# A third Strassen-Winograd step for one more product, and another pair of banks for a small product with ones, in an fp32 kernel on one core

## The chip, the cores and the metric

The kernel runs on one core of a Trainium2 chip. The metric is the device time of the program in microseconds (us). Of the kernel before there are three timed runs, with a median of 429.25 us (429.12 to 429.49), and one profiled execution. A change of less than 0.2% counts as no change here.

## The reference

`x` is 8 sequences of 256 rows of 1024 values. Two layers are added to it, each on its own result:

```python
x = x + _L0_cond_ref(x, itok_B_0_7, W, Wr, A, B)
x = x + einsum('bsi,boi->bso', x, weight[itok_B_0_15])
```

Layer one is a dense product `x @ W.T` (2048 x 1024 by 1024 x 1024) plus a low-rank part: router logits with a bias of 5 on the expert that a sequence's language id names, the two best of eight experts weighted by a softmax, and the projections through `A` and `B` (rank 16 each), times 2. Layer two picks one 1024 x 1024 matrix out of 16 for each sequence by its adapter id. All of it is fp32.

## The kernel before, in words

**Layer one.** The dense product, with an identity added to `W` for the residual, is cut by two Strassen-Winograd steps. The outer step makes seven products out of halves of `W` and `x`; they are called `opening("1", ...)` and `product` with the keys 5, 2, 6, 3, 7, 4, in this order (lines 760 to 816). So key 4 is the last product of layer one, and `adapt(0)`, the first sequence of layer two, comes straight after it. The inner step makes seven products again, P1 to P7, inside `opening` and `product`: `a(i, j)` and `b(i, j)` are quarters of the weight and of the x operand, `s1..s3`, `t1..t3` are their sums on VectorE (`make_subs`), and `late` turns `s2`, `t2` into the fourth sums. Each of the seven goes through `mm` (line 442): two contraction steps times two halves of 128 output rows, each call a matmul of 128 weights' columns by 512 columns. The calls with a third string argument ("0", "1", "d") add the low-rank part with two more such calls, from `hg` and `b_sb` or `bdiff`. P2 is `a(0, 0) b(0, 0)`, P1 is `a(0, 1) b(1, 0)`, and the last one, P4, is `a(1, 1) t2` (line 586).

In keys 5, 2, 3 and 4 (`further` true) P1 is cut a third time: seven matmuls of 128 by 256 columns (helper `deep`, line 513) take the place of four of 512. Their operands `r1..r4`, `q1..q4` are small VectorE sums in pool `sub3`, one buffer for each tag, where `r3`, `q3` take the buffers of `r1`, `q1`. Two of the seven have single banks of their own (`A3`, `B3`), three go straight into the accumulator `X`, and the parts are put together in `dest[:, 0]` by `evict` and `add` on VectorE (lines 547 to 578).

**PSUM.** Eight banks: three pairs, called by the roles A, X and B, and two single banks. `roles` turns the pairs round from one product to the next: the next product's A, X and B are the pairs that were X, B and A. So the pair that key 4 calls A is the B of `adapt(0)`, whose first write into it is `mm("B", s1, w["12"], True)` on line 686.

**Order.** The instruction streams are written out by hand (`manual_schedule`); each engine works through its own in order. VectorE work that is not tied to a product lies in the list `todo` and is given out by `pump(place)`, in shares that depend on what `todo` holds alone; `pump(7)` empties it. For key 4 the list holds the preparation of the first adapter's weights (`prep_w1`) and the y sums (`prep_y`).

**The opening.** `opening` starts TensorE while the loads come in. Its X is in pair 0, its A in pair 1. Warm-up matmuls write `idle`, a tile in pair 2, and so does the product of `ones` with the language ids (line 484), which lays the ids over all partitions. `use_ids` reads it on VectorE (line 200, the comparison that makes `bias`). Then B takes pair 2, and `mm(B, s1, t1)` follows on TensorE.

**Queues.** Weights and x come in over SyncE's DMA queue, in program order; the loads for layer two (`load_w1`) overwrite x and weight blocks and wait until these have been read.

Of the kernel before, what the change touches and what calls it, by code (L numbers as in the profile page):

```python
# [9 lines left out]
F32 = mybir.dt.float32  # L10
# [6 lines left out]
P = 128  # L17
# [8 lines left out]
def kernel(  # L26
# [320 lines left out]
    def us(n):  # L347
        return (n + 151) / 960
# [13 lines left out]
        return pieces(fn, wb[out_], wb[x], wb[y], 2)  # L362

    subs = {}

    def make_subs(key, w, x, further=True):

        def a(i, j):  # L370
            return wb[w][:, 2 * j : 2 * j + 2, i * OQ : (i + 1) * OQ]

        def b(i, j):
            return xb[x][:, 2 * i : 2 * i + 2, j * TQ : (j + 1) * TQ]


        ra = lambda i, j: a(0, 1)[:, j, ts(i, P)]
        rb = lambda i, j: b(1, 0)[:, i, ts(j, TQ // 2)]
        t = {}

        def op3(name, tag, fn, x, y, first=4):
            width = P if name[0] == "r" else TQ // 2

            def run():
                t[name] = sub3.tile([P, width], F32, name=f"{name}_{key}", tag=tag)
                fn(t[name], *(t[v] if isinstance(v, str) else v for v in (x, y)))

            return us(width), first, run

        deep = [  # L390
            op3("r1", "r13", add, ra(1, 0), ra(1, 1)),
            op3("q1", "q13", minus, rb(0, 1), rb(0, 0)),
            op3("r2", "r2", minus, "r1", ra(0, 0)),
            op3("q2", "q2", minus, rb(1, 1), "q1"),
            op3("r4", "r4", minus, ra(0, 1), "r2"),
            op3("q4", "q4", minus, rb(1, 0), "q2"),
        ]

        def deep3():
            for o in (  # L400
                op3("r3", "r13", minus, ra(0, 0), ra(1, 0)),
                op3("q3", "q13", minus, rb(1, 1), rb(0, 1)),
            ):
                o[2]()

        def op(name, fn, x, y, first):
            pool = sub2 if name[1] == "2" else sub1
            width = OQ if name[0] == "s" else TQ

            def run():  # L410
                t[name] = pool.tile([P, 2, width], F32, name=f"{name}_{key}", tag=name)
                fn(t[name], *(t[v] if isinstance(v, str) else v for v in (x, y)))

            return us(2 * width), first, run

        def late_s():
            minus(t["s2"], a(0, 1), t["s2"])

        def late_t():
            minus(t["t2"], b(1, 0), t["t2"])  # L420

        subs[key] = (a, b, t, (late_s, late_t), (ra, rb, deep3), further)
        return [
            op("s1", add, a(1, 0), a(1, 1), 3),
            op("t1", minus, b(0, 1), b(0, 0), 3),
            op("s2", minus, "s1", a(0, 0), 3),
            op("t2", minus, b(1, 1), "t1", 3),
            op("s3", minus, a(0, 0), a(1, 0), 5),
            op("t3", minus, b(1, 1), b(0, 1), 5),
        ] + (deep if further else [])  # L430

    def evict(dest, acc, base=None):

# [24 lines left out]
    def opening(key, dest):  # L458


        idle = pair("idle", 2)
        for i in range(WARM):
            nc.tensor.matmul(idle[:, 0, :P], lhsT=ident, rhs=ident, start=True, stop=True)  # L463
        mm = multiply()
        sums_of = make_subs(key, "11", "11", False)
        a, b, t, late, _, _ = subs.pop(key)
        X = pair(f"X_{key}", 0)
        A = pair(f"A_{key}", 1)
        add_identity(wb["11"], 0, 2)
        mm(X, a(0, 1), b(1, 0), True, part=(0,))  # L470
        project(0, 0, singles("ps_h_0_0"), (2,), last=False)
        mm(X, a(0, 1), b(1, 0), part=(1,))
        evict(dest[:, 0], X)
        project(0, 0, None, (3,), False, False)
        mm(A, a(0, 0), b(0, 0), True, part=(0,))
        project(0, 0, None, (0,), False, False)
        mm(A, a(0, 0), b(0, 0), part=(1,))
        project(0, 0, None, (1,), False, False)
        use_adapter_ids()
        add_identity(wb["11"], 2, 4)  # L480
        for s in sums_of[:4]:
            s[2]()
        add(dest[:, 0], A, dest[:, 0])
        nc.tensor.matmul(idle[:, 1, :NB], lhsT=ones, rhs=ids_f[:, :NB], start=True, stop=True)
        use_ids(idle[:, 1, :NB])
        B = pair(f"B_{key}", 2)
        mm(B, t["s1"], t["t1"], True)
        evict(dest[:, 3], B)
        for s in sums_of[4:]:
            s[2]()  # L490
        mm(A, t["s2"], t["t2"])
        evict(dest[:, 1], A)
        project(0, 0, None, range(KH, KC), False)
        take(0, 0)
        for f in late:
            f()
        mm(A, t["s3"], t["t3"])
        add(dest[:, 3], A, dest[:, 3])
        mm(B, t["s2"], b(1, 1))
        add(dest[:, 1], B, dest[:, 1])  # L500
        mm(A, a(1, 1), t["t2"])
        evict(dest[:, 2], A)

    def product(key, base, dest, lora=None, tokens=None):

        a, b, t, late, (ra, rb, deep3), further = subs.pop(key)
        mm = multiply(dict(zip("01d", b_part(lora))) if lora is not None else None, tokens)
        new = roles(key)
        old = [base[:, q] if base is not None else None for q in range(4)]
        n0, n1 = (slice(j * (TQ // 2), (j + 1) * (TQ // 2)) for j in range(2))  # L510

        def deep(acc, lhs, rhs, first=False):
            nc.tensor.matmul(acc, lhsT=lhs, rhs=rhs, start=first, stop=True, skip_group_check=True)  # L513

        def quarter(m, n):

            return dest[:, 0][:, m, n], old[0][:, m, n] if base is not None else None

        A = new("A")
        mm(A, a(0, 0), b(0, 0), True)  # L520
        X = new("X")
        nc.scalar.copy(X, A)
        if not further:
            pump(1)
            B = new("B")
            mm(B, t["s1"], t["t1"], True, "1", 1)
            evict(dest[:, 3], B, old[3])
            pump(3)
            mm(A, t["s2"], t["t2"])
            evict(dest[:, 1], A, old[1])  # L530
            pump(3)
            mm(X, a(0, 1), b(1, 0), False, "0", 0)
            late[0]()
            late[1]()
            evict(dest[:, 0], X, old[0])
            pump(4)
            mm(A, t["s3"], t["t3"])
            add(dest[:, 3], A, dest[:, 3])
            pump(5)
            mm(B, t["s2"], b(1, 1), False, "d", 1)  # L540
            add(dest[:, 1], B, dest[:, 1])
            pump(6)
            mm(A, a(1, 1), t["t2"], False, "1", 0)
            evict(dest[:, 2], A, old[2])
            pump(7)
            return
        A3 = single(f"A3_{key}", 0)[:, n0]
        deep(A3, ra(0, 0), rb(0, 0), True)
        q, o = quarter(0, n0)
        evict(q, A3, o)  # L550
        pump(1)
        B = new("B")
        mm(B, t["s1"], t["t1"], True, "1", 1, ms=(0,))
        B3 = single(f"B3_{key}", 1)[:, n0]
        deep(B3, t["r1"], t["q1"], True)
        deep3()
        mm(A, t["s2"], t["t2"])
        evict(dest[:, 1], A, old[1])
        deep(A3, t["r2"], t["q2"])
        q, o = quarter(0, n1)  # L560
        evict(q, A3, o)
        late[0]()
        pump(2)
        mm(B, t["s1"], t["t1"], True, "1", 1, ms=(1,))
        evict(dest[:, 3], B, old[3])
        late[1]()
        pump(3)
        deep(X[:, 0, n0], ra(0, 1), rb(1, 0))
        deep(X[:, 0, n1], t["r4"], rb(1, 1))
        deep(X[:, 1, n0], ra(1, 1), t["q4"])  # L570
        mm(X, None, None, False, "0", 0, part=())
        deep(A3, t["r3"], t["q3"])
        two = [P, 2, TQ // 2]
        d1 = dest[:, 0][:, 1, :].rearrange("p (j n) -> p j n", j=2)
        both = A3.unsqueeze(1).to_broadcast(two)
        evict(d1, both, old[0][:, 1, :].rearrange("p (j n) -> p j n", j=2) if base is not None else None)
        add(dest[:, 0][:, :, n1], B3.unsqueeze(1).to_broadcast(two), dest[:, 0][:, :, n1])
        add(dest[:, 0], X, dest[:, 0])
        pump(4)
        mm(A, t["s3"], t["t3"])  # L580
        add(dest[:, 3], A, dest[:, 3])
        pump(5)
        mm(B, t["s2"], b(1, 1), False, "d", 1)
        add(dest[:, 1], B, dest[:, 1])
        pump(6)
        mm(A, a(1, 1), t["t2"], False, "1", 0)
        evict(dest[:, 2], A, old[2])
        pump(7)
# [285 lines left out]
```

## Time and profile before

| What | Value |
|---|---|
| Median of the timed runs | 429.25 us |
| The profiled execution's own time | 430.16 us |
| Its span, first to last instruction | 428.4 us |
| Mean granted TensorE clock | 0.999 |
| TensorE (PE) busy | 423.1 us, 99% |
| VectorE (DVE) busy | 281.7 us, 66% |
| ScalarE (ACT) busy | 39.6 us, 9% |

The profile calls the engines PE (matmul), PEld (TensorE's weight load), DVE, ACT, POOL and SP. One `nc.tensor.matmul` of fp32 is two matmul records and two weight-load records. The recorded length of a matmul overlaps the next one, so the time that one costs is read from the distance between starts. L217 is the line of the helper through which all VectorE sums go, L447 the matmul of `mm`, L513 that of `deep`, L660 that of layer two's `mm`, and L435 ScalarE's copy. In a timeline each line is start, length, engine, line, operation, output<-input and count, with the idle time before it in brackets where there was some.

### The profile page before, as it was taken

Reading aid. Unit: us, or ns where it says so; the run is one execution under the profiler, and the core shown is the slowest. Engines: PE = TensorE matmul, PEld = TensorE weight load, DVE = VectorE, ACT = ScalarE, POOL = GpSimd, SP = SyncE. Lnnn points to the kernel's source line nnn. Section 1 sums busy time; section 2 is a strip of 40 time slices with the busy share of each in tenths; the row PEclk is TensorE's granted clock in tenths of the full one; section 3 lists DMA queues with packets and bytes.
Section 4 is the critical chain, followed back from the end, with each engine's and each line's share of the span. In section 5 each row is a group of like instructions: output and inputs, shape, how many; then the busy total and the mean of one; then the engine's idle time right before and its main releaser. Section 6 shows DMA issues by size and latency. Waiting matters only on the chain.

```text
span 428.4 us, 3335 instructions
## 1 busy us (share of the span) xinstructions
PE 423.1 (99%) x1246; PEld 217.3 (51%) x1246; DVE 281.7 (66%) x375; ACT 39.6 (9%) x65; POOL 2.0 (0%) x10
## 2 busy tenths in 40 slices
PE   8999999999999999999999999999999999999996
PEld 5566984545444445444454444444444444444574
DVE  1627288956988959889595676565756576565531
ACT  1120022110000000000000101010110101010110
POOL 1000000000000000000000000000000000000000
PEclk9999999999999999999999999999999999999999
DMA  8995000000000140630302276556748385550202
GB/s 279 383 398 217 2 0 2 0 0 2 0 0 0 31 168 0 249 142 0 99 0 98 98 262 227 199 207 208 272 148 313 128 275 214 196 197 0 98 2 99
DMA packets 14305, 55.83 MB, mean 130 GB/s; under 512 B 1232, under 2 KB 3536, under 8 KB 9808
## 3 DMA queue, kind: packets, MB, share of 16 engines
q1 hardware_dynamic: 12976, 54.68, 35.5%
q10 hardware_dynamic: 1248, 0.93, 0.7%
q8 instruction: 10, 0.16, 0.2%
q14 instruction: 7, 0.06, 0.0%
q0 software_dynamic: 64, 0.00, 0.0%
HBM read 47.22 MB, written 8.39 MB: 130 GB/s over the span
## 4 chain that ended last, share of the span: by engine, by line
PE 98%; DVE 0%; POOL 0%; issue 0%; ACT 0%; POOLq 0%; DVEq 0%
PE A L447 24%; PE A L660 22%; PE B L447 14%; PE B L660 13%; PE ps_h L245 7%; PE X L660 6%; PE X L447 4%; PE A_last L718 3%; PE A L513 1%; PE X L513 1%; PE idle L463 1%; PE ps_g L315 0%; PE B L513 0%; DVE y L217 0%; ACT z L748 0%
## 5 line engine op out<-in xcount | busy, mean ns | idle before, releaser
L660 PE MATMUL B<-x,x 128*128 128x512 f32 x128 | 57.5, 592 | 0.0
L447 PE MATMUL A<-t,s 128*128 128x512 f32 x112 | 50.3, 592 | 0.0
L217 DVE TENSOR_TENSOR y<-A,y 128x1024 f32<-128x1024 f32 (+2 forms) x27 | 26.3, 985 | 25.1 <-PE A L447 14.2
L660 PE MATMUL A<-w,x 128*128 128x512 f32 x88 | 39.6, 592 | 0.0
L660 PEld LDWEIGHTS B<-x,x 128*128 128x128 f32 x128 | 24.3, 190 | 29.8 <-issue 29.7
L217 DVE TENSOR_TENSOR w<-w,w 128x1024 f32<-128x1024 f32 x24 | 29.0, 1223 | 15.4 <-PE A L660 15.3
L660 PE MATMUL A<-w,y 128*128 128x512 f32 x88 | 39.1, 592 | 0.0
L447 PEld LDWEIGHTS A<-t,s 128*128 128x128 f32 x112 | 21.2, 190 | 22.9 <-issue 22.5
L245 PEld LDWEIGHTS ps_h<-y,x 128*128 128x128 f32 x256 | 30.7, 191 | 3.3 <-issue 3.3
L245 PE MATMUL ps_h<-y,x 128*128 128x136 f32 x256 | 30.6, 279 | 0.0
L660 PEld LDWEIGHTS A<-w,x 128*128 128x128 f32 x88 | 16.7, 190 | 21.0 <-issue 21.0
L660 PEld LDWEIGHTS A<-w,y 128*128 128x128 f32 x88 | 16.7, 190 | 21.0 <-issue 21.0
L435 ACT COPY z<-A 128x512 f32<-128x512 f32 x21 | 12.3, 586 | 158.3 <-PE A L660 158.3
L447 PE MATMUL B<-t,s 128*128 128x512 f32 x56 | 25.9, 594 | 0.3 <-DVE bias L200 0.3
L447 PE MATMUL A<-x,w 128*128 128x512 f32 x56 | 25.3, 592 | 0.0
L447 PE MATMUL A<-t,w 128*128 128x512 f32 x56 | 25.2, 592 | 0.0
L447 PE MATMUL B<-x,s 128*128 128x512 f32 x56 | 25.2, 592 | 0.0
L217 DVE TENSOR_TENSOR y<-B,y 128x1024 f32<-128x1024 f32 (+1 forms) x16 | 17.4, 1090 | 9.5 <-PE B L447 8.7
L217 DVE TENSOR_TENSOR x<-x,x 128x1024 f32<-128x1024 f32 (+1 forms) x20 | 19.2, 1004 | 0.0
L447 PEld LDWEIGHTS B<-x,s 128*128 128x128 f32 x56 | 10.6, 190 | 13.4 <-issue 12.7
L447 PEld LDWEIGHTS A<-t,w 128*128 128x128 f32 x56 | 10.6, 190 | 13.4 <-issue 12.7
L217 DVE TENSOR_TENSOR z<-X,z 128x512 f32<-128x512 f32 x8 | 5.5, 692 | 17.9 <-PE X L660 15.9
(119 smaller groups left out, 446.3 us busy)
## 6 DMA issues: line engine op xcount, KB each, us to landing
x<-w_dram SPq DMA_DIRECT2D x24, 1024.0 KB, 4.8
w<-w_dram SPq DMA_DIRECT2D x8, 1024.0 KB, 4.8
out_dram<-z SPq DMA_DIRECT2D x15, 512.0 KB, 3.0
x<-xT_dram SPq DMA_DIRECT2D x6, 1024.0 KB, 12.9
w<-wT_dram SPq DMA_DIRECT2D x3, 1024.0 KB, 14.9
x<-xT_dram SPq DMA_DIRECT2D x4, 256.0 KB, 3.8
x<-xT_dram SPq DMA_DIRECT2D x2, 512.0 KB, 7.4
w<-w11T_dram SPq DMA_DIRECT2D x1, 512.0 KB, 6.1
```

Of the source, the lines that this page charges most:

```text
L217: nc.vector.tensor_tensor(out_, x, y, op)
L245: nc.tensor.matmul(ps[v][:, u * EA : (u + 1) * EA], lhsT=xk(k, j, c)[:, ts(r, P)], rhs=aw_sb[:, k, :], start=(first and k == some[0] and u ...
L435: nc.scalar.copy(dest, acc)
L447: nc.tensor.matmul(acc[:, m, :], lhsT=l, rhs=r, start=(first and i < len(ms)), stop=(i >= len(steps) - len(ms)), skip_group_check=True,)
L463: nc.tensor.matmul(idle[:, 0, :P], lhsT=ident, rhs=ident, start=True, stop=True)
L513: nc.tensor.matmul(acc, lhsT=lhs, rhs=rhs, start=first, stop=True, skip_group_check=True)
L660: nc.tensor.matmul(accs[name], lhsT=lhs[:, k // 2, k % 2, :], rhs=rhs[:, k, :], start=(first and k == 0), stop=(k == KH - 1), skip_group_c ...
L718: nc.tensor.matmul(acc, lhsT=lhs[:, k // 2, k % 2, :], rhs=rhs[:, k, ts(v, m)], start=(first and k == 0), stop=(k == KH - 1), skip_group_c ...
```

## The change

In P4 of key 4 the third step is applied as it is in P1. The code of the third step moves from `make_subs` and `product` into a function `third`; the keys 5, 2 and 3 keep their instructions and their order. In `opening` the product of ones with the ids goes to a new tile `wide` in pair 0, which the opening's first X has left.

```diff
+    NQ = TQ // 2
+
+    def third(key, lhs, rhs):
+        ra = lambda i, j: lhs()[:, j, ts(i, P)]
+        rb = lambda i, j: rhs()[:, i, ts(j, NQ)]
+        n0, n1 = slice(0, NQ), slice(NQ, TQ)
...
+        ops = [
+            op("r1", "r13", add, A(1, 0), A(1, 1)),
+            op("q1", "q13", minus, B(0, 1), B(0, 0)),
+            op("r2", "r2", minus, "r1", A(0, 0)),
+            op("q2", "q2", minus, B(1, 1), "q1"),
+            op("r4", "r4", minus, A(0, 1), "r2"),
+            op("q4", "q4", minus, B(1, 0), "q2"),
+        ]
+
+        def ops3():
+            op("r3", "r13", minus, A(0, 0), A(1, 0))[2]()
+            op("q3", "q13", minus, B(1, 1), B(0, 1))[2]()
+
+        def piece(n, acc=None):
+            if n in (1, 5):
+                own[n] = single(f"P{n}_{key}", n // 5)[:, n0]
+            out_, l, r = {
+                1: lambda: (own[1], ra(0, 0), rb(0, 0)),
+                2: lambda: (acc[:, 0, n0], ra(0, 1), rb(1, 0)),
+                3: lambda: (acc[:, 0, n1], t["r4"], rb(1, 1)),
+                4: lambda: (acc[:, 1, n0], ra(1, 1), t["q4"]),
+                5: lambda: (own[5], t["r1"], t["q1"]),
+                6: lambda: (own[1], t["r2"], t["q2"]),
+                7: lambda: (own[1], t["r3"], t["q3"]),
+            }[n]()
+            nc.tensor.matmul(out_, lhsT=l, rhs=r, start=(n in (1, 5)), stop=True, skip_group_check=True)
+
+        def take(n, dest, base=None):
+            cut = lambda v: {1: v[:, 0, n0], 6: v[:, 0, n1], 5: v[:, :, n1]}[n]
+            if n == 7:
+                cut = lambda v: v[:, 1, :].rearrange("p (j n) -> p j n", j=2)
+            src = own[5 if n == 5 else 1]
+            if n in (5, 7):
+                src = src.unsqueeze(1).to_broadcast([P, 2, NQ])
+            evict(cut(dest), src, None if base is None else cut(base))
+
+        return ops, ops3, piece, take
...
-        nc.tensor.matmul(idle[:, 1, :NB], lhsT=ones, rhs=ids_f[:, :NB], start=True, stop=True)
-        use_ids(idle[:, 1, :NB])
+        wide = pair("ids_wide", 0)[:, 0, :NB]
+        nc.tensor.matmul(wide, lhsT=ones, rhs=ids_f[:, :NB], start=True, stop=True)
+        use_ids(wide)
         B = pair(f"B_{key}", 2)
         mm(B, t["s1"], t["t1"], True)
...
+        two = key == "4"
+        _, ops3, piece, take = deep
...
+        piece(7)
+        take(7, dest[:, 0], old[0])
+        take(5, dest[:, 0], dest[:, 0])
+        if two:
+            ops, ops3, piece, take = third(f"{key}b", lambda: a(1, 1), lambda: t["t2"])
+            for o in ops:
+                o[2]()
         add(dest[:, 0], X, dest[:, 0])
         pump(4)
         mm(A, t["s3"], t["t3"])
         add(dest[:, 3], A, dest[:, 3])
+        if two:
+            piece(1)
+            take(1, dest[:, 2], old[2])
         pump(5)
         mm(B, t["s2"], b(1, 1), False, "d", 1)
+        if two:
+            piece(5)
+            ops3()
+            piece(6)
+            take(6, dest[:, 2], old[2])
         add(dest[:, 1], B, dest[:, 1])
         pump(6)
+        if two:
+            mm(A, None, None, False, "1", 0, part=())
+            for n in (2, 3, 4):
+                piece(n, A)
+            piece(7)
+            take(7, dest[:, 2], old[2])
+            take(5, dest[:, 2], dest[:, 2])
+            add(dest[:, 2], A, dest[:, 2])
+            pump(7)
+            return
         mm(A, a(1, 1), t["t2"], False, "1", 0)
         evict(dest[:, 2], A, old[2])
         pump(7)
```

More of the change, by code (lines that the diff above doesn't have):

```diff
@@ L364, with op, run @@
     subs = {}
+    NQ = TQ // 2
[3 more added lines that the diff above has]
+        n0, n1 = slice(0, NQ), slice(NQ, TQ)
+        t, own = {}, {}
+        def op(name, tag, fn, x, y):
+            width = P if name[0] == "r" else NQ
+            def run():
+                t[name] = sub3.tile([P, width], F32, name=f"{name}_{key}", tag=tag)
+                fn(t[name], *(t[v] if isinstance(v, str) else v() for v in (x, y)))
+            return us(width), 4, run
+        A, B = (lambda i, j: lambda: ra(i, j)), (lambda i, j: lambda: rb(i, j))
+        ops = [
[31 more added lines that the diff above has]
+        return ops, ops3, piece, take
     def make_subs(key, w, x, further=True):
@@ L374, in b @@
             return xb[x][:, 2 * i : 2 * i + 2, j * TQ : (j + 1) * TQ]
-        ra = lambda i, j: a(0, 1)[:, j, ts(i, P)]
-        rb = lambda i, j: b(1, 0)[:, i, ts(j, TQ // 2)]
         t = {}
[L381 to L404, printed above, removed]
         def op(name, fn, x, y, first):
@@ L420, in late_t @@
             minus(t["t2"], b(1, 0), t["t2"])
-        subs[key] = (a, b, t, (late_s, late_t), (ra, rb, deep3), further)
+        deep = third(key, lambda: a(0, 1), lambda: b(1, 0)) if further else None
+        subs[key] = (a, b, t, (late_s, late_t), deep)
         return [
@@ L429, in make_subs @@
             op("t3", minus, b(1, 1), b(0, 1), 5),
-        ] + (deep if further else [])
+        ] + (deep[0] if further else [])
     def evict(dest, acc, base=None):
@@ L465, in opening @@
         sums_of = make_subs(key, "11", "11", False)
-        a, b, t, late, _, _ = subs.pop(key)
+        a, b, t, late, _ = subs.pop(key)
         X = pair(f"X_{key}", 0)
@@ L504, in product @@
     def product(key, base, dest, lora=None, tokens=None):
-        a, b, t, late, (ra, rb, deep3), further = subs.pop(key)
+        a, b, t, late, deep = subs.pop(key)
         mm = multiply(dict(zip("01d", b_part(lora))) if lora is not None else None, tokens)
@@ L509, in product @@
         old = [base[:, q] if base is not None else None for q in range(4)]
[L510 to L517, printed above, removed]
         A = new("A")
@@ L522, in product @@
         nc.scalar.copy(X, A)
-        if not further:
+        if deep is None:
             pump(1)
@@ L546, in product @@
             return
[L547 to L550, printed above, removed]
+        two = key == "4"
+        _, ops3, piece, take = deep
+        piece(1)
+        take(1, dest[:, 0], old[0])
         pump(1)
@@ L553, in product @@
         mm(B, t["s1"], t["t1"], True, "1", 1, ms=(0,))
-        B3 = single(f"B3_{key}", 1)[:, n0]
-        deep(B3, t["r1"], t["q1"], True)
-        deep3()
+        piece(5)
+        ops3()
         mm(A, t["s2"], t["t2"])
         evict(dest[:, 1], A, old[1])
-        deep(A3, t["r2"], t["q2"])
-        q, o = quarter(0, n1)
-        evict(q, A3, o)
+        piece(6)
+        take(6, dest[:, 0], old[0])
         late[0]()
@@ L567, in product @@
         pump(3)
-        deep(X[:, 0, n0], ra(0, 1), rb(1, 0))
-        deep(X[:, 0, n1], t["r4"], rb(1, 1))
-        deep(X[:, 1, n0], ra(1, 1), t["q4"])
+        for n in (2, 3, 4):
+            piece(n, X)
         mm(X, None, None, False, "0", 0, part=())
[L572 to L577, printed above, removed]
+        piece(7)
[5 more added lines that the diff above has]
+                o[2]()
         add(dest[:, 0], X, dest[:, 0])
@@ L581, in product @@
         add(dest[:, 3], A, dest[:, 3])
+        if two:
+            piece(1)
+            take(1, dest[:, 2], old[2])
         pump(5)
         mm(B, t["s2"], b(1, 1), False, "d", 1)
+        if two:
+            piece(5)
+            ops3()
+            piece(6)
+            take(6, dest[:, 2], old[2])
         add(dest[:, 1], B, dest[:, 1])
         pump(6)
+        if two:
+            mm(A, None, None, False, "1", 0, part=())
+            for n in (2, 3, 4):
+                piece(n, A)
[5 more added lines that the diff above has]
+            return
         mm(A, a(1, 1), t["t2"], False, "1", 0)
```

## The prediction

> **What bounds the kernel now.** I read the page's busy shares first, then the chain that ended last, then the waits of TensorE, and then the timeline at the two places that the change touches. The page, with the line of busy times and the line of the chain by engine:
>
> ```profile
> PE 423.1 (99%) x1246; PEld 217.3 (51%) x1246; DVE 281.7 (66%) x375; ACT 39.6 (9%) x65; POOL 2.0 (0%) x10
> ...
> PE 98%; DVE 0%; POOL 0%; issue 0%; ACT 0%; POOLq 0%; DVEq 0%
> ```
>
> TensorE sets the end: whatever shortens its stream comes off the time, and VectorE work costs something only where TensorE comes to wait for it. TensorE's waits, in the view of who waited for whom, are two:
>
> ```profile
> PE idle L463 <- POOL ident masks.py:199: 1.4, 1, 1.4
> PE B L447 <- DVE bias L200: 0.3, 1, 0.3
> ```
>
> The second is at one of the places of the change. The timeline there, weight loads, matmuls and VectorE from three answers:
>
> ```profile
> 16.66 0.29 PEld L484 LDWEIGHTS idle<-ids_f,ones 1*128 1x128 f32 x2
> 17.36 0.30 PEld L447 LDWEIGHTS B<-t,s 128*128 128x128 f32 x2 [0.41 <-DVE bias L200]
> ...
> 16.67 0.38 PE L484 MATMUL idle<-ids_f,ones 1*128 1x8 f32 x2
> 17.37 1.55 PE L447 MATMUL B<-t,s 128*128 128x512 f32 x3 [0.32 <-DVE bias L200]
> ...
> 17.09 0.23 DVE L200 TENSOR_TENSOR bias<-idle,ecol 128x64 f32<-128x64 f32 x1
> ```
>
> B's first weight load stands still until the comparison on VectorE has read the ids out of B's pair, 17.09 + 0.23 = 17.32 us. The other place is key 4. TensorE there, and VectorE:
>
> ```profile
> 215.18 0.59 PE L513 MATMUL X<-x,w 128*128 128x256 f32 x2
> 215.61 0.59 PE L513 MATMUL X<-x,r 128*128 128x256 f32 x2
> 216.04 0.59 PE L513 MATMUL X<-q,w 128*128 128x256 f32 x2
> ...
> 218.62 3.60 PE L447 MATMUL A<-t,s 128*128 128x512 f32 x8
> 222.06 3.60 PE L447 MATMUL B<-x,s 128*128 128x512 f32 x8
> 225.49 1.88 PE L447 MATMUL B<-hg,bdiff 128*128 128x512 f32 x4
> 227.21 3.60 PE L447 MATMUL A<-t,w 128*128 128x512 f32 x8
> 230.64 1.88 PE L447 MATMUL A<-hg,b_sb 128*128 128x512 f32 x4
> 232.35 3.60 PE L660 MATMUL A<-w,y 128*128 128x512 f32 x8
> 235.79 3.60 PE L660 MATMUL B<-x,x 128*128 128x512 f32 x8
> ```
>
> ```profile
> 219.05 0.69 DVE L217 TENSOR_TENSOR y<-A,y 128x512 f32<-128x512 f32 x1
> 219.77 0.69 DVE L217 TENSOR_TENSOR y<-B,y 128x512 f32<-128x512 f32 x1
> 220.49 1.22 DVE L217 TENSOR_TENSOR y<-X,y 128x1024 f32<-128x1024 f32 x1
> ...
> 227.41 1.23 DVE L217 TENSOR_TENSOR y<-B,y 128x1024 f32<-128x1024 f32 x1 [2.29 <-PE B L447]
> ...
> 232.56 1.23 DVE L217 TENSOR_TENSOR y<-A,y 128x1024 f32<-128x1024 f32 x1 [2.60 <-PE A L447]
> ```
>
> No TensorE line has a bracket. The starts give the costs: a call of 512 columns is 3.43/4 = 0.858 us (222.06 to 225.49), one of 256 columns 0.43 us (215.18 to 215.61), half. VectorE stands idle 2.29 and 2.60 us before the last two.
>
> **The Trainium skill.** "TensorE: Matmul & The Clock Gate", section "Step-by-step: what each phase is for", has matmuls in program order with only weight loads pulled ahead. The trace agrees: in a 512-column row a weight load of 0.19 us starts 0.43 us before its matmul. The same page, "LDWEIGHTS", makes a load's time depend on the columns alone, not on rows: the ids' one-row load takes 0.182 us, a 128-row load 0.190. "PSUM — Partial Sum Buffer", section "PSUM bank collisions raise a hardware error", forbids two engines in one bank at once and asks for a guard by bank. B's wait is this guard at work: the ids are in the second bank of pair 2, and B needs both.
>
> **Part one: P4 in seven pieces.** Removed on TensorE: 4 x 0.858 = 3.43 us. Added: 7 x 0.43 = 3.01 us. The two low-rank calls (1.72 us) stay. That is 0.42 us less, if no piece waits. I lay the new streams out. TensorE, from the end of A's P at 222.06 (times without the opening's shift): piece 1 at 222.06, B's P 222.49, its low rank 225.92, piece 5 at 227.64, piece 6 at 228.07, low rank of A 228.50, pieces 2, 3, 4 at 230.21, 230.64, 231.07, piece 7 at 231.50, `adapt(0)` at 231.93 in place of 232.35.
>
> VectorE gets 13 instructions for one. Starts in a row give their cost: r 0.20, q about 0.35, so the six sums of the first batch took 1.65 us in the row from 193.55 to 195.20; `take` of 256 columns 0.34 (recorded 0.42), a `take` of 512 elements 0.72; the last add costs what the evicting one did. Added: 1.65 + r3, q3 0.55 + take 1 and 6 0.68 + take 7 and 5 1.44 = 4.3 us. Each against its reader:
> - The six sums start at 220.49 behind take 5 of P1, whose buffers and operands are free by then. The X add ends at 223.3, not 221.7; nobody needs that pair before `adapt(0)`. One pumped piece follows, then the add into `dest[:, 3]` to 225.6, then take 1 to 225.9. The low rank of A needs the former at 228.50, piece 6 the latter at 228.07: 2.2 us to spare. The next pumped piece ends at 227.0.
> - r3 must wait for piece 5. A VectorE reader starts 0.63 us after the start of a 256-column piece (208.31 to 208.94 in P1), so 228.27; r3, q3 and take 6 end at 229.2. Queued behind: B's add into `dest[:, 1]`, to 230.3 (227.41 before), and two y sums, to 231.7. Piece 7 needs r3, q3 and take 6 at 231.50: 2.3 us to spare.
> - take 7 starts at 231.50 + 0.63 = 232.13, take 5 at 232.85, the A add at 233.57 and ends at 234.79. Before, it ended at 233.79. This is what is late next: `adapt(0)`'s B takes this pair. Its first weight load would start at 235.36 - 0.43 = 234.93 and can start as late as 235.36 - 0.19 = 235.17. So 0.14 to 0.4 us of cover remains where there was 2 us; I put the stall at 0. If take 7 starts later, the cost is one for one beyond that.
> - Behind, two more y sums and the two pieces of `w["11"]` end some 1.0 us later, near 238.2; `adapt(0)` needs the latter at 245.7. VectorE idles 1.35 us at 241.14 and 2.28 us at 246.36 in the row of before, so the lag is gone there.
>
> ScalarE has no part in it. SyncE's load over key 4's x block was issued at 225.68, after B's P had read it; piece 1 puts that off 0.43 us, against a preparation that reads it from 246.97 on and a landing time of 4.8 us. No other DMA is moved.
>
> **Part two: the ids in pair 0.** No instruction is added or removed. The new wait, for pair 0, has been satisfied since ScalarE's copy of X ended at 11.57; pair 0 is next written by the projection at 38.3. B's weight load may follow the ids' loads. By TensorE's record 0.32 us is won; by the weight loads' own idle time, 0.41; if the third load follows the second at the pitch of these two (16.66, 16.77) it starts at 16.88 in place of 17.36, 0.48. That no earlier instruction holds B is seen from `t1`, ready at 13.4, and the t2 sum, done at 15.14. I take 0.41, range 0.3 to 0.48. Behind it TensorE has no visible wait on a transfer; the nearest one on VectorE is `W`'s last-but-one block, issued about 22 and landing after a median 14.9 us, so near 37, read at 37.86. If VectorE then waits 0.4 us, it idles 3.57 us before 45.96 anyway.
>
> **The sum.** 0.42 + 0.41 = 0.83 us. The profiled span goes from 428.4 to 427.57, with 430.16 - 428.4 = 1.76 us around it to 429.33. That execution was 0.91 us above the median of the runs; the same 0.83 off 429.25 gives 428.42, or 428.4. A measurement of this kernel tells about 0.2%, 0.86 us, from no change: the forecast lies just inside that line.
>
> **Rivals.** (a) The pair's handover stalls. The VectorE tail above is tight to 0.14 us; if it begins 0.5 us late, say as the pumped y sums run longer in front of take 7 (their slack is 0.4 us), B waits about 0.3 us: 428.7. Against: P1 shows the same takes at these prices. (b) The opening's gain is given back at a later wait, so part one stands alone: 428.83. For: loads fill the queue until 38 us. Against: TensorE waits for no load after 4.25. (c) P4's gain fails, and only the opening's is left: 428.84. For: sums through one-buffer tags tie the engines together twice. Against: margins above 2 us. (d) Slower: the weight loads of 256-column calls come out from under the matmuls. A load of 0.19 stands in a pitch of 0.215, so only 0.025 is free. Fourteen loads of 0.19 fully exposed are 2.66 us, 429.25 - 0.83 + 2.66 = 431.1. It decides above 0.83 + 0.86 = 1.69 us, that is 0.12 us a load. Against: pieces 2, 3, 4 of P1 stand at 0.43 in a row.
>
> **How the numbers follow.** Forecast 0.75, (a) 0.08, (b) 0.05, (c) 0.04, (d) 0.08. The forecast's own range is 0.72 to 0.90 us gained, with 0.15 for the medians 428.2 to 428.7; 0.42 of its chance lies beyond the line of 0.2% and 0.33 within. (a), (b), (c) fall within. So faster 0.42, same 0.50, slower 0.08. The range of 428.1 to 429.0 takes in (a), (b), (c) and leaves out (d).
>
> **What would show it.** Right: no wait of B on `bias`, B's first load near 16.9; seven L513 pieces in steps of 0.43 in P4; P4's work from A's P to `adapt(0)` 13.3 us for 13.7 (218.62 on); no bracket on L660's first B; the A add ending just before B's first load. Wrong: a TensorE wait on a VectorE y or r line near 228, 231 or 235, or piece steps above 0.43.

## The result, and the profile after

Twenty runs of each: 428.56 us after (427.82 to 429.33) against 429.43 us before (428.75 to 430.16). The ratio is 0.998 with a 95% interval of 0.9973 to 0.9987: 0.87 us less, where 0.83 was forecast. The gain is 0.203%, on the line of 0.2% itself; the interval lies wholly below 1, so the kernel is faster, but it is not shown that it is faster by more than 0.2%. The interval allows a gain of 0.56 to 1.16 us; the traces below are sharper.

The page of the changed kernel, its busy times and its chain by engine (helpers have new line numbers: `mm` is L479, the pieces L411, layer two's `mm` L700, the ids' product L517):

```profile
PE 422.2 (99%) x1252; PEld 218.3 (51%) x1252; DVE 285.7 (67%) x387; ACT 39.6 (9%) x65; POOL 2.0 (0%) x10
...
PE 99%; POOL 0%; ACT 0%; issue 0%; POOLq 0%
```

TensorE is busy for 0.9 us less, in six records more: 0.41 us less from the opening's B on, and 0.42 less in the first microseconds, which the change doesn't touch. VectorE is busy for 4.0 us more in twelve instructions more, and VectorE has gone out of the chain. Of TensorE's two waits, in the view of who waited for whom, one is left:

```profile
PE idle L495 <- POOL ident masks.py:199: 1.4, 1, 1.4
```

In the opening, TensorE's weight loads (start, length, engine, line, operation):

```profile
15.23 0.89 PEld L245 LDWEIGHTS ps_h<-y,x 128*128 128x128 f32 x7 [0.24 <-issue]
16.25 0.29 PEld L517 LDWEIGHTS ids_wide<-ids_f,ones 1*128 1x128 f32 x2
16.56 0.30 PEld L479 LDWEIGHTS B<-t,s 128*128 128x128 f32 x2
```

B's first load comes 1.33 us after the last group of the projection and has no bracket. Before it came 17.36 - 15.65 = 1.71 us after it: 0.38 us are won. In key 4, TensorE's matmuls from the product with `s3` and `t3` to layer two:

```profile
217.82 3.60 PE L479 MATMUL A<-t,s 128*128 128x512 f32 x8
221.25 0.59 PE L411 MATMUL P_4b<-t,w 128*128 128x256 f32 x2
...
226.83 1.03 PE L411 MATMUL P_4b<-q_4b,r_4b 128*128 128x256 f32 x4
227.69 1.88 PE L479 MATMUL A<-hg,b_sb 128*128 128x512 f32 x4
...
230.71 0.59 PE L411 MATMUL P_4b<-q_4b,r_4b 128*128 128x256 f32 x2
231.14 3.60 PE L700 MATMUL A<-w,y 128*128 128x512 f32 x8
234.57 3.60 PE L700 MATMUL B<-x,x 128*128 128x512 f32 x8
```

From 217.82 to 231.14 are 13.32 us, where there were 232.35 - 218.62 = 13.73: 0.41 us won, and nothing waits. VectorE's tail of P4, and the weight load of the first B of layer two, which takes the pair that the last add frees:

```profile
231.34 1.42 DVE L217 TENSOR_TENSOR y<-P_4b,y 128x512 f32<-128x512 f32 x2 [0.46 <-PE P_4b L411]
232.79 1.22 DVE L217 TENSOR_TENSOR y<-A,y 128x1024 f32<-128x1024 f32 x1
...
234.14 0.19 PEld L700 LDWEIGHTS B<-x,x 128*128 128x128 f32 x1 [0.24 <-issue]
```

The add ends at 232.79 + 1.22 = 234.01, 0.13 us before that load.

The profiled span is 1.3 us shorter (427.1 for 428.4), but only 0.38 + 0.41 = 0.79 of that belongs to the change. Another 0.42 us lies ahead of both places: the last projection group starts at 15.23 for 15.65, and most of that is in the first four matmul records of X, 3.17 us to the next group's start (4.13 to 7.30) where the trace of before has 3.46 (4.25 to 7.71). (The last 0.1 us is rounding.) The change touches nothing there. It is why stretches are compared below by distances between starts, not by times from the span's start.

One such stretch takes in both places of the change and leaves the first microseconds out: from the start of the opening's last projection group to the first matmul of layer two. It is 232.35 - 15.65 = 216.70 us before and 231.14 - 15.23 = 215.91 us after, 0.79 less. It is called the long stretch below.

### The profile page after: what moved, and what is told of

Read it like the earlier page. It is cut to its first block, busy times and chain, and to the rows that moved or that the text cites. A ratio compares the mean times of both kernels' runs of the same rounds, so it can differ in the third digit from the quotient of the medians.

```text
span 427.1 us, 3361 instructions
## 1 busy us (share of the span) xinstructions
PE 422.2 (99%) x1252; PEld 218.3 (51%) x1252; DVE 285.7 (67%) x387; ACT 39.6 (9%) x65; POOL 2.0 (0%) x10
## 4 chain that ended last, share of the span: by engine, by line
PE 99%; POOL 0%; ACT 0%; issue 0%; POOLq 0%
PE A L479 23%; PE A L700 23%; PE B L479 15%; PE B L700 13%; PE ps_h L245 7%; PE X L700 6%; PE X L479 4%; PE A_last L758 3%; PE P L411 2%; PE X L411 1%; PE idle L495 1%; PE ps_g L315 0%; PE P_4b L411 0%; PE A L411 0%; ACT z L788 0%
## 5 line engine op out<-in xcount | busy, mean ns | idle before, releaser
L700 PE MATMUL B<-x,x 128*128 128x512 f32 x128 | 57.5, 592 | 0.0
L479 PE MATMUL A<-t,s 128*128 128x512 f32 x112 | 50.3, 592 | 0.0
L700 PE MATMUL A<-w,x 128*128 128x512 f32 x88 | 39.6, 592 | 0.0
L700 PEld LDWEIGHTS B<-x,x 128*128 128x128 f32 x128 | 24.3, 190 | 29.8 <-issue 29.7
L700 PE MATMUL A<-w,y 128*128 128x512 f32 x88 | 39.1, 592 | 0.0
L479 PEld LDWEIGHTS A<-t,s 128*128 128x128 f32 x112 | 21.2, 190 | 22.9 <-issue 22.5
L217 DVE TENSOR_TENSOR y<-A,y 128x1024 f32<-128x1024 f32 x18 | 22.0, 1221 | 15.0 <-PE A L479 11.7
L700 PEld LDWEIGHTS A<-w,x 128*128 128x128 f32 x88 | 16.7, 190 | 21.0 <-issue 21.0
L700 PEld LDWEIGHTS A<-w,y 128*128 128x128 f32 x88 | 16.7, 190 | 20.6 <-issue 20.6
L479 PE MATMUL B<-t,s 128*128 128x512 f32 x56 | 25.9, 594 | 0.0
L479 PE MATMUL A<-x,w 128*128 128x512 f32 x56 | 25.3, 592 | 0.0
L479 PE MATMUL B<-x,s 128*128 128x512 f32 x56 | 25.2, 592 | 0.0
L479 PE MATMUL A<-t,w 128*128 128x512 f32 x48 | 21.6, 592 | 0.0
L217 DVE TENSOR_TENSOR y<-B,y 128x1024 f32<-128x1024 f32 x12 | 14.6, 1219 | 6.5 <-PE B L479 6.5
L217 DVE TENSOR_TENSOR t<-x 128x1024 f32<-128x1024 f32 x14 | 17.0, 1217 | 0.5 <-DMA x<-xT_dram 0.5
L479 PEld LDWEIGHTS B<-x,s 128*128 128x128 f32 x56 | 10.6, 190 | 13.0 <-issue 12.2
```

Source lines behind the costliest of these rows:

```text
L217: nc.vector.tensor_tensor(out_, x, y, op)
L479: nc.tensor.matmul(acc[:, m, :], lhsT=l, rhs=r, start=(first and i < len(ms)), stop=(i >= len(steps) - len(ms)), skip_group_check=True,)
L700: nc.tensor.matmul(accs[name], lhsT=lhs[:, k // 2, k % 2, :], rhs=rhs[:, k, :], start=(first and k == 0), stop=(k == KH - 1), skip_group_c ...
```

## The experiments

Theory: the change is two independent gains on TensorE's stream, the wait for B's pair, and an eighth of P4's columns (seven calls of 256 for four of 512); VectorE's 4.3 us are hidden, with little to spare at the pair's handover. The rivals are those of the prediction.

**Each part alone.** The ids' part in the kernel before:

```diff
-        nc.tensor.matmul(idle[:, 1, :NB], lhsT=ones, rhs=ids_f[:, :NB], start=True, stop=True)
-        use_ids(idle[:, 1, :NB])
+        wide = pair("ids_wide", 0)[:, 0, :NB]
+        nc.tensor.matmul(wide, lhsT=ones, rhs=ids_f[:, :NB], start=True, stop=True)
+        use_ids(wide)
```

> The kernel before with the ids' product in pair 0, and P4 as it was. Theory (two independent parts, 0.4 us each): from the start of the last projection group of the opening to B's first weight load 1.33 us as in the changed kernel (1.71 before), no wait of B on the comparison; the time 0.4 us below before (ratio 0.999). From key 4's A product with s3 and t3 to the first matmul of layer two 13.73 us, as before. Rival (b), the opening's gain is given back later: TensorE shows a new wait of about 0.4 us between 17 and 62 us and the time is that of before. Rival (the gain is all in the ids' part): the time falls by 0.8 us.

And the same edit undone in the changed kernel, which leaves P4's part:

> The changed kernel with the ids' product put back into pair 2, so P4 in seven pieces alone. Theory: from the product with s3 and t3 to layer two 13.32 us (13.73 before), no wait of TensorE there; B's wait of 0.32 us on the comparison is back; the time 0.4 us below before (ratio 0.999). Rival (c), P4 gives nothing: 13.7 us and the time of before.

Measured: the ids alone 428.94 us against 429.44 (ratio 0.9987, interval 0.9979 to 0.9994), P4 alone 429.06 (ratio 0.9994, 0.9985 to 1.0002). By the medians these are 0.50 and 0.38 us, by the ratios 0.56 and 0.26, though P4's interval reaches just over 1: the times alone don't show P4's part. The traces do. With the ids alone, B's first load stands 1.33 us after the projection's group, TensorE has no wait but the warm-up's, and the stretch of key 4 is 230.41 - 216.68 = 13.73 us. With P4 alone it is 232.00 - 218.67 = 13.33 us, and the old wait is back:

```profile
PE B L479 <- DVE bias L200: 0.3, 1, 0.3
```

The long stretch is 230.41 - 14.09 = 216.32 us with the ids alone and 232.00 - 15.70 = 216.30 with P4 alone: 0.38 and 0.40 less than before, 0.78 in sum, for 0.79 with both. So the parts add up, neither is given back, and rivals (b) and (c) fall.

**What B waits for.** The comparison that reads the ids is put behind the sums `s3`, `t3` on VectorE, once with the ids in pair 2 (the kernel before), once in pair 0 (the changed one):

```diff
-        use_ids(...)
-        B = pair(f"B_{key}", 2)
-        mm(B, t["s1"], t["t1"], True)
-        evict(dest[:, 3], B)
         for s in sums_of[4:]:
             s[2]()
+        use_ids(...)
+        B = pair(f"B_{key}", 2)
+        mm(B, t["s1"], t["t1"], True)
+        evict(dest[:, 3], B)
```

> The kernel before with the comparison that reads the ids put behind the sums s3 and t3 on VectorE (0.60 + 1.14 us more in front of it), the ids still in pair 2. Theory (B waits because the ids lie in its own pair): B's first weight load starts some 1.75 us later, at about 3.45 us after the last projection group instead of 1.71, and TensorE shows a wait on the comparison of about 2.1 us; the time is 1.7 us above before. Rival (the 0.3 us are the seam after a one-row product, whatever VectorE does): the wait stays at 0.3 us.

> The changed kernel with the same delay of the comparison, the ids in pair 0. Theory: B does not wait, its first load stays 1.33 us after the last projection group, and the time is that of the changed kernel, 0.8 us below before. Rival (B still depends on VectorE's progress through some other tile): a wait of up to 1.7 us comes back.

TensorE's weight loads, first with pair 2, then with pair 0:

```profile
17.73 0.30 PEld L447 LDWEIGHTS B<-t,s 128*128 128x128 f32 x2 [2.11 <-DVE bias L200]
```

```profile
16.08 0.29 PEld L517 LDWEIGHTS ids_wide<-ids_f,ones 1*128 1x128 f32 x2
16.39 0.30 PEld L479 LDWEIGHTS B<-t,s 128*128 128x128 f32 x2
```

In pair 2 B's load follows 3.42 us after the projection's group (it started at 14.31), for 1.71: the wait has grown by VectorE's 1.7 us, as the theory has it. In pair 0 it stays at 1.33 us (15.06 to 16.39) and the run took 428.74 us, near the changed kernel's 428.56. The pair is the cause, not the seam after a one-row product. (One execution of each.)

But the run with pair 2 took 432.22 us, 2.8 above before and not 1.7, and its long stretch is 234.41 - 14.31 = 220.10 us, 3.40 more than before. The table of stretches shows where the rest went (length, then busy time with count for PE, PEld, DVE, ACT and POOL, then the granted clock, the DMA share and GB/s); this is the stretch after the wait:

```profile
17.70:20.00 2.30, 2.27 (x4) 1.09 (x5) 0.20 (x1) 0.00 (x0) 0.00 (x0) 0.73 1.05 386
```

The granted clock is 0.73 here. In slices of half a microsecond it is 1.00 up to 18.7 us, 0.50 to 0.55 from there to 22.2, and 1.00 again: it fell 1 us after TensorE had resumed its work and stayed down for about 3.4 us. B's product takes 5.23 us (17.73 to 22.96), where it took 3.53 before (17.37 to 20.90). To see whether the idle time did this, TensorE was kept busy in front of B:

```diff
+        filler = pair("filler", 0)
+        for i in range(9):
+            nc.tensor.matmul(filler[:, 0, :P], lhsT=ident, rhs=ident, start=True, stop=True)
         B = pair(f"B_{key}", 2)
```

> The kernel before with the late comparison (ids in pair 2), and nine unused products of the identity with itself into pair 0 (they belong to no output) in front of B, which keep TensorE busy for about 1.9 of the 2 us in which B waits. Theory (the time beyond the wait in the run with the late comparison came from a lower granted clock, which followed from TensorE standing idle): the granted clock stays at 1.00 between 17 and 24 us where it was 0.73, and B's product takes 3.4 us from first to next and not 5.2; the time is about 1 us lower, near 431.2. Rival (the lower clock has nothing to do with the idle time): 0.73 again.

The same stretch, with the filler:

```profile
17.70:20.00 2.30, 2.30 (x15) 1.77 (x14) 1.24 (x3) 0.00 (x0) 0.00 (x0) 1.00 1.05 386
```

The clock stays at 1.00 and B's product takes 3.52 us (18.82 to 22.34). The time, one run of 431.58 us, is only 0.64 lower; but this run's projection group had started 1.07 us later in the span (15.38 for 14.31), and 0.64 + 1.07 = 1.71 us is what B's product got back. The long stretch says the same: 233.79 - 15.38 = 218.41 us, 1.71 above before, which is the wait alone. So an idle time of 2.0 us (2.1 between the weight loads) cost 1.7 us over and above itself, in the one execution that there is of it. The Trainium skill, "TensorE: Matmul & The Clock Gate", section "What's actually happening", lets the clock fall to half after an idle window of about 3.4 us; here an idle time of 2.0 us was enough. Whether every idle time of this length does it was not tried.

**The cover at the handover.** One sum, then three sums, of 128x512 into an unused buffer, ahead of the last add:

```diff
             take(5, dest[:, 2], dest[:, 2])
+            for i in range(1):      # and range(3)
+                minus(sub1.tile([P, 2, OQ], F32, name=f"spare{i}", tag="s3"), a(0, 0), a(1, 0))
             add(dest[:, 2], A, dest[:, 2])
```

> The changed kernel with one more VectorE sum of 128x512 into an unused buffer ahead of the last add of P4 (the output is not touched). It delays that add, which frees the pair that layer two's first B takes, by about 0.6 us. Theory: the changed kernel has 0.13 us until B's first weight load and at most 0.24 us more until it hurts, so TensorE shows a new wait of 0.2 to 0.5 us at L660's B, now on VectorE's last add. Rival (TensorE does not need this pair so soon, the cover is 1 us or more): no wait.

> The same with three such sums, some 1.8 us of delay. Theory: one for one beyond the cover, so the wait at B is 1.2 us more than with one sum, 1.4 to 1.7 us in all, and the time is up by as much. Rival (part of the delay is taken up elsewhere): less than 1 us more than with one sum.

Matmuls of layer two, with one sum, then with three:

```profile
231.00 3.60 PE L702 MATMUL A<-w,y 128*128 128x512 f32 x8
234.45 3.67 PE L702 MATMUL B<-x,x 128*128 128x512 f32 x8
237.96 1.45 PE L702 MATMUL A<-w,x 128*128 128x512 f32 x3
```

```profile
230.01 3.60 PE L702 MATMUL A<-w,y 128*128 128x512 f32 x8
234.92 3.67 PE L702 MATMUL B<-x,x 128*128 128x512 f32 x8 [1.31 <-issue]
238.43 1.02 PE L702 MATMUL A<-w,x 128*128 128x512 f32 x2
```

From the first A to the second are 6.96 us with one sum and 8.42 with three, where 234.57 + 3.43 - 231.14 = 6.86 is free of waits: losses of 0.10 and 1.56 us. The add ended 2.87 us after layer two's start in the changed kernel, 3.35 with one sum (233.13 + 1.22 - 231.00) and 4.81 with three (233.60 + 1.22 - 230.01). So the loss begins at 3.25, and from there it is one for one. The cover left by the change is 0.38 us, the upper end of the 0.14 to 0.4 that was forecast. The loss with one sum was under the 0.2 to 0.5 us expected: the sum delays the add by 0.48 us only, not 0.6, since the add reads what take 5 has just written and starts 0.12 us later for it when nothing lies between (the start of take 7 to that of the add is 1.45 us in the changed kernel, to that of the spare sum 1.33). A y sum that reads the one before it shows the same: it starts 0.72 us after it (229.47 to 230.19 in the changed kernel), one that doesn't 0.60 (233.93 to 234.53). With three sums the profile puts the wait down to "issue"; that VectorE's add ends 0.1 us before B's matmul tells what it was. The times of the two runs, 428.89 and 429.34 us, are only 0.45 apart, for layer two began 0.99 us earlier in the second (230.01 for 231.00); the sum of these, 1.44, is near the 1.46 between the losses.

**Weight loads.** Each piece of key 4's P4 in two calls of 128 columns:

```diff
-            nc.tensor.matmul(out_, lhsT=l, rhs=r, start=(n in (1, 5)), ...)
+            for c in cols:      # two halves of 128 columns
+                nc.tensor.matmul(out_[:, c], lhsT=l, rhs=r[:, c], start=first, ...)
```

> The changed kernel with each of the seven pieces of key 4's P4 in two calls of 128 columns with the same weights, 28 weight loads in place of 14. Theory (a call's cost follows its columns down to 128, since loads stand 0.114 us apart in the projections of 136 columns): the stretch from the product with s3 and t3 to layer two is 13.32 us, at most 0.2 us more. Rival (d) (a load of 0.19 us must fit under its own matmul): each of the 28 records then costs 0.19 instead of 0.107 us, 5.3 us in place of 3.0, and the stretch is 15.6 us.

```profile
217.96 3.60 PE L482 MATMUL A<-t,s 128*128 128x512 f32 x8
...
231.38 3.60 PE L703 MATMUL A<-w,y 128*128 128x512 f32 x8
```

13.42 us with 28 loads, 0.10 more than with 14 (one run, of 429.18 us). Rival (d) falls, with room to spare.

**The same step in more products.** P4 cut a third time in keys 2 and 3 as well:

```diff
-        two = key == "4"
+        two = key in "234"
```

> The changed kernel with P4 cut a third time in keys 2, 3 and 4. Theory (a third step of one product saves 0.41 us on TensorE wherever VectorE has the 4.3 us to give): two more times 0.41 us where there is room, so 0.8 us below the changed kernel and 1.65 below before (ratio 0.996). Rival (VectorE is too full in keys 2 and 3, where it is 80 to 90% busy in some slices): TensorE waits appear on the y or r lines of VectorE there, and the time is above that of the changed kernel.

430.38 us, ratio 1.0026 (1.0017 to 1.0034): slower than both kernels. TensorE's waits:

```profile
PE B L479 <- DVE y L217: 1.6, 2, 1.1
...
PE P_2b L411 <- DVE y L217: 0.4, 1, 0.4
```

The two waits of B, 0.57 us behind key 2 and 1.08 behind key 3, are at the handover of the pair. There the cover of 0.38 us isn't left, since pumped sums stand in front of the takes: take 7 starts 1.79 us after piece 7 in key 2 (122.35 to 124.14) and 2.29 in key 3 (177.27 to 179.56), for 0.63 in key 4. The view of waits understates the loss, as a matmul's recorded length (0.59 us for a pitch of 0.43) runs over into the wait. Behind key 3, where two products take 6.87 us without a wait, the starts are

```profile
177.70 3.60 PE L479 MATMUL A<-x,w 128*128 128x512 f32 x8
182.37 3.67 PE L479 MATMUL B<-t,s 128*128 128x512 f32 x8 [1.08 <-DVE y L217]
185.88 3.60 PE L479 MATMUL A<-t,s 128*128 128x512 f32 x8
```

8.18 us apart: 1.31 lost. Behind key 2 it is 7.68 (122.78 to 130.46), 0.81 lost. Pieces 1 and 6 of key 2 lose another 0.77 us. With 0.82 gained by the columns this makes 2.07 us more than in the changed kernel, and the long stretch is 233.12 - 15.15 = 217.97 us, 2.06 more. If the handover is what key 3 lost, the pair can be freed sooner, for A is complete before piece 7:

```diff
             piece(7)
-            take(7, dest[:, 2], old[2])
-            take(5, dest[:, 2], dest[:, 2])
-            add(dest[:, 2], A, dest[:, 2])
+            add(dest[:, 2][:, 0], A[:, 0], dest[:, 2][:, 0])
+            add(dest[:, 2][:, 1], A[:, 1], old[2][:, 1])
+            take(7, dest[:, 2], dest[:, 2])
+            take(5, dest[:, 2], dest[:, 2])
```

> P4 cut a third time in keys 3 and 4, and in both the accumulator A is added first in the tail (in two halves), ahead of the takes of pieces 7 and 5, so that its pair comes free about 1.3 us sooner. Theory (what key 3 lost with three keys cut is the handover of this pair, 1.08 us, and not VectorE's load as such): no wait of TensorE at the next product's B, 0.41 us below the changed kernel, 1.25 below before (ratio 0.997). Rival (VectorE, all but full from 165 to 205 us, is the bound there): the wait moves to another line of VectorE, and the time is that of the changed kernel or above.

> The same with P4 of key 2 cut too. Theory: the handover's 0.57 us in key 2 goes as in key 3; the wait of 0.39 us of key 2's piece 6 on take 1 stays, since it lies ahead of the tail. So 0.82 - 0.39 = 0.43 us below the changed kernel, as with keys 3 and 4 alone. Rival (VectorE's load is the bound, 37.4 of 40 us busy from 100 to 140): waits of 0.5 us or more on other lines, and the time is above that of the changed kernel.

Keys 3 and 4 so: 428.05 us, ratio 0.9971 (0.9962 to 0.998) to before, 1.5 us under it and 0.4 to 0.5 under the changed kernel, and TensorE waits for nothing after the warm-up. The long stretch is 230.19 - 14.70 = 215.49 us, 0.42 below the changed kernel's. VectorE's load is no obstacle in itself: in the stretch from 165 to 205 us it is busy for all but 0.21 us.

```profile
165.00:205.00 40.00, 40.00 (x103) 19.25 (x102) 39.79 (x53) 1.99 (x2) 0.00 (x0) 1.00 0.31 108
```

With key 2 too: 428.39 us, ratio 0.9976 (0.9968 to 0.9985). The handover's wait has gone, and 0.39 us at key 2's piece 6 are left, as expected; but the expected 0.43 us below the changed kernel are not there. The long stretch is 230.29 - 14.44 = 215.85 us, 0.06 below the changed kernel's and 0.36 above that with keys 3 and 4 alone; the medians are 0.34 apart, though the intervals overlap. The expectation took the wait as the view lists it. By the starts, pieces 5 and 6 of key 2

```profile
117.11 0.59 PE L411 MATMUL P_2b<-q_2b,r_2b 128*128 128x256 f32 x2
118.10 0.70 PE L411 MATMUL P_2b<-q_2b,r_2b 128*128 128x256 f32 x2 [0.39 <-DVE y L217]
118.63 1.88 PE L479 MATMUL A<-hg,b_sb 128*128 128x512 f32 x4
```

take 1.52 us for 0.86, 0.66 lost, and piece 1 takes 0.53 (111.43 to 111.96) for 0.43. That is 0.76 against a gain of 0.41: in key 2 the step costs 0.35 us. The changed kernel was not timed beside these two; by time, the gain of keys 3 and 4 over it rests on each one's ratio to before (0.9971 and 0.998 are 0.4 us apart, the medians 0.5).

## Why the prediction was right

- **TensorE sets the end.** Right: both gains came through whole, and VectorE's four extra microseconds cost nothing.
- **The sum.** Forecast 0.83 us, in the traces 0.41 + 0.38 = 0.79. That the medians say 0.87 is as much luck as measurement, with an interval of 0.56 to 1.16. The median of 428.56 us lies above the 428.4 forecast; the kernel before, timed beside it, came out 0.18 us higher too (429.43 for 429.25).
- **P4 at 0.42 us.** Measured 0.41; pieces stand at 0.43, as costed from P1.
- **The ids at 0.41 us, 0.3 to 0.48.** Measured 0.38. The upper bound, the pitch of the two ids' loads, doesn't hold: B's load starts 0.31 us after the first of them (16.25 to 16.56), not 0.22.
- **The wait at B's pair.** Right in what B waits for, the comparison that reads the ids. But "B needs both" banks doesn't describe it: the ids lay in the second bank, B's first matmul writes the first (`mm` takes the halves in turn), and already its weight load stood still until 17.36, just after the comparison's end at 17.32. The two banks are one tile in the program, and it was this tile as a whole that was waited for. A guard by single banks was not tried.
- **VectorE's row.** Relative to the start of layer two the last add was laid out to end at 234.79 - 231.93 = 2.86 us; it ended at 2.87. Take 7 was to start 0.63 us after piece 7 and did (230.71 to 231.34). The first six sums took 1.61 us for 1.65.
- **The handover, what is late next.** Named with a cover of 0.14 to 0.4 us; it is 0.38. (The "2 us" of cover before are too round: the add ended at 233.79, so 1.57 us before B's load at 235.36, and 1.81 before the latest start on the same reckoning.) This is the step that decided: in keys 2 and 3 the same edit, without that cover, made the kernel slower. Rival (a) had the mechanism, pumped sums that put take 7 off; in key 4 they were done 0.46 us before take 7 could start.
- **Rival (d)** was argued badly, though it had little chance. "Only 0.025 is free" took the recorded length of a load for what it occupies; the kernel before has loads 0.116 us apart in its projections (not 0.114, as an expectation has it), and the run with 128 columns shows that more than 0.1 of the 0.215 us is free.
- **The slower case was named in the wrong place.** Weight loads could not do it. The pair's handover can, for which rival (a) allowed 0.3 us only: with three extra sums it lost 1.56 us, with keys 2, 3 and 4 2.1 us.

## What to carry to other kernels

Where one engine is busy for 99% of the span, cost an edit by distances between starts on that engine, then follow the other engine's work up to the instruction that frees the next buffer: a gain is safe as far as that one has cover, and the cover can be measured by putting spare work in front of it. When a new tail is in the way, free what the next stage needs first, then do what only the result needs. What a wait costs is read from the starts too: at the handovers and at key 2's piece 6 the wait that the view lists is 0.2 to 0.3 us short of the loss. A small read that shares a pair of banks with a big accumulator can cost a wait of its own; here another pair that was free took it away.

## What was not expected of the hardware

- TensorE standing idle for 2.0 us from 15.7 us on was followed, 1 us after it had resumed, by a granted clock of one half for about 3.4 us; B's product took 5.23 us for 3.53. With TensorE kept busy the clock stayed at 1.00, and so it did after an idle time of 1.31 us before layer two (three sums). Each of these is one execution.
- A recorded weight load of 0.19 us takes at most about 0.11 us of TensorE's stream: 14 calls of 128 columns with 28 loads cost 0.10 us more than 7 of 256 with 14.
- The first four matmul records of X, the same in all kernels here, took from 1.97 us (the ids alone, 4.19 to 6.16) to 3.46 (before) up to the next group's start. They begin at half pace, though the table of stretches gives a granted clock of 1.00 there: in the trace of before their weight loads stand 0.86 us apart (5.26, 6.12, 6.97), those of X's second half 0.43 (9.07, 9.50); in that of the ids alone they are 0.43 apart from 4.87 on. So a difference of up to 1.5 us between single executions tells nothing of a change here, while the long stretch of kernels with the same work agrees to 0.01 us (215.91 in the changed kernel, 215.91 in that with the late ids in pair 0).
